# A four-layer graph-attention kernel: two ties at a layer border, row stores on another queue, a last half by position, a root on GpSimd

## The chip, the cores and the metric

The kernel runs on one core of one Trainium2 chip. The metric is the device time of one execution in microseconds, the median of several. The times here are 2258.48, 2259.3 and 2261.46 us.

## The reference

A graph of N = 4096 nodes with F = 256 features passes four attention layers. Each layer is followed by a residual sum and a layer norm: `x = layernorm(x + layer(x))`. The adjacency matrix is random with density 1/256 and a full diagonal, so that a node has some 17 neighbours. Layers 0 and 1 have four heads, layer 2 has two. The last layer, which the change touches most, is

```python
h = x @ W
e = leaky_relu(h @ a[:F] + (h @ a[F:]).T, 0.2)
attention = softmax(where(adj > 0, e, -1e12), axis=1)
negative = -softmax(where(adj > 0, -e, -1e12), axis=1)
out = elu(concatenate([attention @ x, negative @ x], axis=1) @ fc_W)
x = layernorm(x + out)        # (x - mean) / sqrt(var + 1e-5)
```

## The kernel before

**Tiling.** The nodes form 32 row tiles of 128. For each row tile, a first stage packs the neighbours of its 128 rows into 13 tiles of gathered nodes; with the tile's own rows this makes NP = 14 positions, two halves of HALF = 7. For a layer, every node has a row in DRAM (`vals`), made by the `Projection` (L529) of the layer before: the transposed row block times the weights, with the steps transpose, copy, multiply, row (which stores `vals` at L583), edge (a transpose on PE, L587) and store (L595).

**A row tile** (`RowTile`, L604). `load` (L630) fetches in half 0 the attention terms S (L635) and the mask mk (L637), in half 1 the residual rows y (L1012), all on SP's queue. Of the 14 positions it gathers 13 by GpSimd's indirect DMA (L645); position FRONT = 6 is the tile's own rows and comes by a plain load on SP (L642). `place` (L613) gives each position a slot of a pool that other tiles use again. `half` (L649) computes, in layer 3, seven Relus of 128x128 on ScalarE (L686), an Exp of 128x896 (L687), a multiplication by the mask on VectorE (L688), a second Exp (L689), a second multiplication (L690), and 14 matmuls on TensorE (L723) into two banks. `finish` (L741, L1060) scales the two sums (L1054, L1057, L1074 to L1076), applies the ELU (L1079 to L1082, with an Exp on ScalarE at L1080) and calls `norm` (L1015): statistics (L1022, L1023), variance plus epsilon (L1031), the inverse root by a bit trick (L1033, L1034) and three Newton steps of four instructions each (L1038 to L1041), the scaling of the row (L1043), and its store on SP's queue (L1045). In layer 3 the store goes to the output.

**Whole rows.** In layers 2 and 3 some blocks of four row tiles are not gathered: they are computed against all 32 node tiles. In layer 3 these are rows 28 to 31, in 64 units of four matmuls (L993), each with a Relu (L985), an Exp (L987 or L989), a mask (L990) and a load of node rows (vw, L970). The other 28 row tiles (0 to 27) go by gather. The units are spread over the steps (`whole`), with AHEAD = 10 of them before the first half.

**Order.** A scheduler orders the instructions of each engine by priority within the program's data dependences, and each engine executes its own list in order; that holds of SP's queue, too, whose list is loads and stores. `tc.issue_after(ins)` pins the instructions of a block behind `ins` on the engine of `ins`. `half_with_whole` (L839) is one step of layers 2 and 3: the half of a tile, projections, the finish of the tile before, units.

**The border.** `close` (L889) ends a layer. Between layers 2 and 3 it loads the first four tiles of layer 3, runs five of its units, finishes the last row tile of layer 2, projects it, pins tile 0's first half and five more units behind the scaling of that row (on VectorE) and the last transpose of its projection (on TensorE), and calls tile 1's first half without a pin. At the end of layer 3 it runs the units that are left and finishes tile 27.

Of the kernel before, what the change touches and what calls it, by code (L numbers as in the profile page):

```python
# [37 lines left out]
F32 = mybir.dt.float32  # L38
# [6 lines left out]
AF = mybir.ActivationFunctionType  # L45
ALU = mybir.AluOpType
# [4 lines left out]
P = 128  # L51
# [4 lines left out]
BT = 4  # L56
# [17 lines left out]
HALF = NP // 2  # L74
# [10 lines left out]
WIDTH = (65, 65, 129, 257)  # L85
VALS = tuple(h * w for h, w in zip(HEADS, WIDTH))
# [4 lines left out]
TERMS = tuple(a + b for a, b in zip(LOGS, EXPS))  # L91
# [8 lines left out]
AHEAD = 10  # L100
# [38 lines left out]
@with_exitstack  # L139
def kernel(ctx: ExitStack, tc: tile.TileContext, ins: dict, out: bass.AP):  # L140
    nc = tc.nc
    const = ctx.enter_context(tc.tile_pool(name="const", bufs=1))
    dram = ctx.enter_context(tc.tile_pool(name="xs", bufs=1, space=DRAM))
    ident = const.tile([P, P], F32, name="ident")
    make_identity(nc, ident)
    shared = {
        "ident": ident,
        "idx": const.tile([P, NT, NP], I32, name="idx"),
        "flag": const.tile([1, 1], I32, name="flag"),
        "shift1": const.tile([P, 1], F32, name="shift1"),  # L150
        "shift2": const.tile([P, 1], F32, name="shift2"),
        "shift3": const.tile([4, 4], F32, name="shift3"),
        "zero": const.tile([4, 4], F32, name="zero"),
        "maskC": dram.tile([NT, P, NP, MC], U8, name="maskC"),
        "maskW": dram.tile([NB, P, NT, BT, MC], U8, name="maskW"),
        "d": [const.tile([P, NT, TERMS[n]], F32, name=f"d{n}") if WHOLE[n] else None for n in range(4)],
        "v": [dram.tile([N, ROW[n]], F32, name=f"vals{n}") for n in range(4)],
        "e": [dram.tile([NT, TERMS[n], P], F32, name=f"edge{n}") for n in range(4)],
        "x": [None] + [dram.tile([N, F], F32, name=f"xp{n}") for n in (1, 2, 3)],
    }  # L160
    nc.vector.memset(shared["shift1"], -KEXP)
    nc.vector.memset(shared["shift2"], -2.0 * KEXP)

    nc.vector.memset(shared["zero"], 0.0)
    nc.vector.memset(shared["shift3"], -2.0 * KEXP)
    nc.gpsimd.affine_select(out=shared["shift3"], in_=shared["shift3"], pattern=[[1, 4]], compare_op=ALU.is_gt,
                            fill=0.0, base=0, channel_multiplier=-1)
    with ExitStack() as packed:
        Program(tc, packed, ins, out, shared).run()
    general = nc.values_load(shared["flag"][0:1, 0:1], min_val=0, max_val=1,  # L170
                             skip_runtime_bounds_check_because="it is the result of a comparison")
    with tc.If(general > 0):
        dense_layers(tc, ins, out, ident)
# [430 lines left out]
class RowTile:  # L604
# [44 lines left out]
    def half(self, half):  # L649
# [32 lines left out]
            return G[k][:, V + T + h:V + T + h + 1]  # L682

        if n == 3:
            for k in range(HALF):
                nc.scalar.activation(w[0][:, k, :], S[:, 0, :], AF.Relu, bias=d(k, 0))  # L686
            nc.scalar.activation(w[1], w[0], AF.Exp, scale=-1.0)  # L687
            nc.vector.tensor_tensor(w[1], w[1], mh, op=ALU.mult)  # L688
            nc.scalar.activation(w[0], w[0], AF.Exp, bias=sh["shift2"])  # L689
            nc.vector.tensor_tensor(w[0], w[0], mh, op=ALU.mult)  # L690
            heads = (1, 0)
        else:
            for h in range(A, T):
                k = 0
                while k < HALF:
                    pos = half * HALF + k
                    e = 2 if pos % 2 == 0 and k + 1 < HALF else 1
                    if e == 2:
                        dd = self.slots[pos // 2][:, :2 * ROW[n]].rearrange("p (t c) -> p t c", t=2)
                        nc.vector.tensor_tensor(  # L700
                            w[h][:, k:k + 2, :], S[:, h:h + 1, :].to_broadcast([P, 2, P]),
                            dd[:, :, V + T + h:V + T + h + 1].to_broadcast([P, 2, P]), op=ALU.mult)
                    else:
                        nc.vector.tensor_scalar(w[h][:, k, :], S[:, h, :], d(k, h), None, op0=ALU.mult)
                    k += e
            for h in range(A):
                for k in range(HALF):
                    nc.scalar.activation(w[h][:, k, :], S[:, h, :], AF.Exp, bias=d(k, h))  # L708
                if n == 2:
                    nc.vector.scalar_tensor_tensor(w[h], w[h], LEAST, mh, op0=ALU.max, op1=ALU.mult)  # L710
                elif h % 2 == 0:
                    masked(pairs[h // 2])
            heads = list(range(A, H)) + list(range(A))
        for h in heads:
            for k in range(HALF):
                pos = half * HALF + k
                how = dict(start=pos == 0 and (n == 3 or h == heads[0]), stop=pos == NP - 1, skip_group_check=True)
                v = G[k][:, h * Wd:(h + 1) * Wd]
                if n < 2:
                    nc.tensor.matmul(accs[0][:Wd, h * P:(h + 1) * P], v, w[h][:, k, :], **how)  # L720
                else:
                    a = accs[h][:, :Wd] if n == 3 else accs[0][:, h * Wd:(h + 1) * Wd]
                    nc.tensor.matmul(a, w[h][:, k, :], v, **how)  # L723

    def copy(self):

# [19 lines left out]
class Layer:  # L746
# [3 lines left out]
    def __init__(self, prog, n):  # L750
        self.prog, self.n, self.nc, self.shared = prog, n, prog.nc, prog.shared
        self.order = ORDER[n]
        self.count = len(self.order)
        self.tiles = {}
        self.loaded = set()
        self.units = self.whole_rows()
        self.total = len(WHOLE[n]) * NT * (1 if n < 3 else 2)
        self.used = self.ahead = 0
        self.nxt = self.middle = self.between = None
        self.stored = []  # L760
        self.group = []
        self.ready = []
        self.step = 0
        self.last = ()
# [74 lines left out]
    def half_with_whole(self, m, part):  # L839
# [12 lines left out]
        with ExitStack() as order:  # L852
            for ins in self.last:
                order.enter_context(self.prog.tc.issue_after(ins))
            self.last = ()
            if part == 1 or self.tile(m).accs is None:
                self.tile(m).half(part)
        if self.between is not None:

            self.last = self.between()  # L860
            self.between = None
# [8 lines left out]
        for proj in projs:  # L870
            proj.row()
            proj.edge()
        self.stored = projs

    def steps(self):
        for m in range(self.count):
# [12 lines left out]
    def close(self, following):  # L889
# [16 lines left out]
        if WHOLE[self.n]:  # L906
            for _ in self.units:
                pass
            if following is None:
                self.tile(last).finish()  # L910
                return


            following.ahead = AHEAD
            self.project_ready()
            for _ in range(AHEAD // 2):
                following.unit()
            self.tile(last).finish()
            scaled = self.scaled
# [1 line left out]
            with ExitStack() as order:  # L921
                for ins in (scaled, proj.last):
                    order.enter_context(self.prog.tc.issue_after(ins.ins))
                following.tile(0).half(0)
                for _ in range(AHEAD - AHEAD // 2):
                    following.unit()
        else:
            self.set_banks()
            first = Projection(self.prog, self.n + 1, self.nxt, *self.ready.pop(0)[1:])
# [11 lines left out]
        if following is not None:  # L941
            for m in (1, 2):
                following.load(m, 0)
            following.tile(1).half(0)
            following.load(3, 0)


# [67 lines left out]
    def norm(self, y, m):  # L1015
# [13 lines left out]

        v = ep.tile([P, BT], F32, name="v")[:, :g]  # L1030
        nc.vector.tensor_scalar(v, mv[:, :, 1], EPS, None, op0=ALU.add)  # L1031
        b = ep.tile([P, BT], I32, name="b")[:, :g]
        nc.vector.tensor_scalar(b, v.bitcast(I32), 1, None, op0=ALU.logical_shift_right)  # L1033
        nc.vector.tensor_scalar(b, b, -1.0, float(0x5F3759DF), op0=ALU.mult, op1=ALU.add)  # L1034
# [2 lines left out]
        for _ in range(3):  # L1037
            nc.vector.tensor_tensor(u, r, r, op=ALU.mult)  # L1038
            nc.vector.tensor_tensor(u, u, v, op=ALU.mult)  # L1039
            nc.vector.tensor_scalar(u, u, -0.5, 1.5, op0=ALU.mult, op1=ALU.add)  # L1040
            nc.vector.tensor_tensor(r, r, u, op=ALU.mult)  # L1041
        for i, (y, m) in enumerate(self.group):
            self.scaled = nc.vector.tensor_scalar(y, y, mv[:, i, 0:1], r[:, i:i + 1], op0=ALU.subtract, op1=ALU.mult)  # L1043
            dst = self.prog.out if self.n == 3 else self.shared["x"][self.n + 1]
            nc.sync.dma_start(out=dst[m * P:(m + 1) * P, :], in_=y)  # L1045
            if self.n < 3:
                self.ready.append((self.step + 1, y, m))
        self.group = []

# [495 lines left out]
```

## Time and profile before

| what | value |
|---|---|
| median of three runs | 2259.3 us |
| profiled execution, own time | 2261.27 us |
| profiled execution, span | 2259.5 us |
| mean granted TensorE clock | 0.963 of full speed |
| busy: PE, PEld | 2020.2, 1842.9 us |
| busy: DVE, ACT, POOL | 1786.0, 1730.1, 1493.1 us |
| 1456 gathers (L645) on POOL | 1480.1 us busy, 1017 ns each |
| layer 3, first full gather to the end | 1767.8 to 2259.5 us |

The profile is one execution, and its times are microseconds from the start of the span. PE is TensorE's matmuls, PEld its weight loads, DVE VectorE, ACT ScalarE, POOL GpSimd, SP SyncE; SPq is SP's queue of DMAs. In a line of a group or timeline, `w<-S,G` says that a tile named w is written from S and G; L686 is line 686 of the kernel before. Idle time in brackets, as in `[8.56 <-DMA G<-vals]`, is the time that the engine stood ahead of the instruction, and what released it. The ends of matmuls are modelled, and POOL's spans are rough. All four layers use every engine, so a share of the whole span says little on the last layer.

### The profile page before, as it was taken

How to read it: one execution, taken by the hardware profiler on the slowest of the kernel's cores; microseconds unless marked ns; L12 is line 12 of the kernel's file. 1: busy time of each engine (PE TensorE's matmuls, PEld its weight loads, DVE VectorE, ACT ScalarE, POOL GpSimd, SP SyncE). 2: the span in 40 equal slices, each digit the busy share in tenths (PEclk: the TensorE clock that was granted, in tenths of full speed). 3: DMA queues.
4: the chain of work that ended last, by engine and by line, in shares of the span. 5: the costliest groups of instructions: out<-in, count | busy, mean ns of one | idle time of the engine just before them, and what ended most of it. 6: DMA issues, size and time to landing. Idle time of an engine off the chain costs nothing. (4 is left out here: it accounts for less than half of the span.)

```text
span 2259.5 us, 49108 instructions
## 1 busy us (share of the span) xinstructions
PE 2020.2 (89%) x15689; PEld 1842.9 (82%) x15689; DVE 1786.0 (79%) x5061; ACT 1730.1 (77%) x4977; POOL 1493.1 (66%) x1596
## 2 busy tenths in 40 slices
PE   4878888989999969989889898999998999899995
PEld 2658878878899859988889798999997888788784
DVE  2888999999999859888889786887976466655566
ACT  4777988988789859978889767987875666666653
POOL 2107656656667777777777777777773477777773
PEclk7898999999999979999999999999999999999998
DMA  8779868776567666666666666778777688898874
GB/s 283 250 242 357 281 214 255 251 245 225 147 169 193 178 197 171 180 179 168 175 182 168 171 166 182 211 216 235 227 220 212 197 281 273 261 284 261 260 239 122
DMA packets 250319, 492.99 MB, mean 218 GB/s; under 512 B 44385, under 2 KB 156610, under 8 KB 249666
## 3 DMA queue, kind: packets, MB, share of 16 engines
q0 software_dynamic: 81536, 245.30, 38.4%
q1 hardware_dynamic: 168514, 244.46, 33.7%
q8 instruction: 126, 2.06, 0.4%
q14 instruction: 143, 1.17, 0.2%
HBM read 437.05 MB, written 52.54 MB: 217 GB/s over the span
## 5 line engine op out<-in xcount | busy, mean ns | idle before, releaser
L645 POOL DMA_INDIRECT G<-vals,idx x1456 | 1480.1, 1017 | 723.2 <-issue 225.1
L708 ACT ACTIVATE w<-S,G 128x128 f32<-128x128 f32 x3248 | 1000.1, 390 | 137.9 <-DMA G<-vals,idx 99.6
L720 PE MATMUL bank<-w,G 128*65 128x128 f32 x7168 | 840.7, 277 | 61.0 <-DVE w L679 61.0
L720 PEld LDWEIGHTS bank<-w,G 128*65 128x65 f32 x7168 | 801.9, 141 | 70.8 <-DVE w L679 69.5
L679 DVE SCALAR_TENSOR_TENSOR w<-w,bank 128x1792 f32<-128x1792 f32 x256 | 514.7, 2014 | 16.6 <-ACT w L708 14.2
L723 PE MATMUL bank<-G,w 128*128 128x257 f32 (+1 forms) x2688 | 495.7, 342 | 33.7 <-ACT z L1057 21.6
L723 PEld LDWEIGHTS bank<-G,w 128*128 128x128 f32 x2688 | 436.0, 195 | 82.7 <-ACT z L1057 26.1
L993 PE MATMUL bank<-vw,pw 128*128 128x129 f32 (+1 forms) x2048 | 301.2, 304 | 1.8 <-issue 1.8
L993 PEld LDWEIGHTS bank<-vw,pw 128*128 128x128 f32 x2048 | 276.4, 193 | 17.8 <-issue 2.3
L686 ACT ACTIVATE w<-S,G 128x128 f32<-128x128 f32 x392 | 137.2, 391 | 148.6 <-DMA G<-vals 94.6
L438 DVE TENSOR_SCALAR oh<-iota,place 128x256 bf16<-128x256 f16 (+2 forms) x992 | 222.6, 300 | 9.7 <-PE bank L444 9.7
L700 DVE TENSOR_TENSOR w<-S,G 128x256 f32<-128x256 f32 x384 | 152.4, 417 | 69.9 <-DMA G<-vals,idx 66.8
L444 PE MATMUL bank<-mk,oh 128*128 128x132 fp8e4 x2336 | 191.3, 227 | 15.6 <-DVE oh L438 9.3
L555 PE MATMUL bank<-wext,xT 128*128 128x268 f32 (+3 forms) x640 | 180.8, 416 | 15.6 <-ACT xT L546 12.8
L444 PEld LDWEIGHTS <-oh 128*128 128x128 bf16 x2336 | 147.6, 99 | 51.0 <-DVE oh L438 16.2
L383 ACT ACTIVATE mk<-raw 128x1024 uint8<-128x1024 int32 x128 | 130.5, 1051 | 29.6 <-DMA raw<-in_adjB_dram 29.6
L555 PEld LDWEIGHTS bank<-wext,xT 128*128 128x128 f32 x640 | 119.6, 204 | 35.4 <-ACT xT L546 15.6
L983 DVE SCALAR_TENSOR_TENSOR pw<-pw,mw 128x512 f32<-128x512 f32 x192 | 127.4, 689 | 18.0 <-ACT pw L982 17.7
L982 ACT ACTIVATE pw<-Sw,d 128x512 f32<-128x512 f32 x192 | 133.0, 709 | 8.6 <-PE bank L993 5.5
L688 DVE TENSOR_TENSOR w<-w,mk 128x896 f32<-128x896 f32 x56 | 61.0, 1090 | 96.3 <-ACT w L687 87.6
L710 DVE SCALAR_TENSOR_TENSOR w<-w,mk 128x896 f32<-128x896 f32 x80 | 86.7, 1087 | 39.8 <-ACT w L708 39.6
L451 ACT ACTIVATE cm<-bank 128x396 uint8<-128x396 f32 (+1 forms) x160 | 69.0, 452 | 47.4 <-PE bank L444 46.3
(130 smaller groups left out, 1519.3 us busy)
## 6 DMA issues: line engine op xcount, KB each, us to landing
raw<-in_adjB_dram SPq DMA_DIRECT2D x128, 512.0 KB
mk<-maskC SPq DMA_DIRECT2D x112, 231.0 KB
G<-vals,idx POOLq DMA_INDIRECT x1456
S<-edge SPq DMA_DIRECT2D x64, 256.0 KB
vw<-vals SPq DMA_DIRECT2D x96, 129.0 KB
xp<-y SPq DMA_DIRECT2D x96, 128.0 KB
y<-xp SPq DMA_DIRECT2D x96, 128.0 KB
mw<-maskW SPq DMA_DIRECT2D x20, 528.0 KB
```

The lines of the kernel that those rows point to most:

```text
L438: nc.vector.tensor_scalar(oh[:, :n * P], iota[:, :n * P], self.place[:, it, j:j + 1], None, op0=ALU.is_equal)
L444: nc.tensor.matmul(accs[b][:, s * MC:(s + 1) * MC], oh[:, (k - a) * P:(k - a + 1) * P], mk[:, j, it, :].bitcast(FP8), start=touches[b][0] ...
L555: nc.tensor.matmul(pp[:, :c1 - c0], self.xT[:, k, :], wext[:, k, c0:c1], start=(k == 0), stop=(k == KT - 1 and brow is None))
L645: nc.gpsimd.indirect_dma_start(out=self.place(pos), out_offset=None, in_=sh["v"][n][:NODES[t], :], in_offset=bass.IndirectOffsetOnAxis(ap= ...
L679: nc.vector.scalar_tensor_tensor(pair, pair, LEAST, mh2, op0=ALU.max, op1=ALU.mult)
L686: nc.scalar.activation(w[0][:, k, :], S[:, 0, :], AF.Relu, bias=d(k, 0))
L700: nc.vector.tensor_tensor(w[h][:, k:k + 2, :], S[:, h:h + 1, :].to_broadcast([P, 2, P]), dd[:, :, V + T + h:V + T + h + 1].to_broadcast([P ...
L708: nc.scalar.activation(w[h][:, k, :], S[:, h, :], AF.Exp, bias=d(k, h))
L720: nc.tensor.matmul(accs[0][:Wd, h * P:(h + 1) * P], v, w[h][:, k, :], **how)
L723: nc.tensor.matmul(a, w[h][:, k, :], v, **how)
L982: nc.scalar.activation(p, S[:, h], AF.Exp, bias=d)
L993: nc.tensor.matmul(accs[it][:, c:c + Wd], p[:, it, :], v[:, c:c + Wd], start=(j == 0 and h == heads[0]), stop=(j == NT - 1), skip_group_ch ...
```

## The change

1. A constant tile `mhalf` of -0.5 is added, with one memset.
2. At the border of layers 2 and 3, three units instead of five run ahead of the last row's finish, seven instead of five behind it, and tile 1's first half is pinned behind the same two instructions as tile 0's.
3. The 32 output rows of layer 3 are stored by ScalarE's queue instead of SP's. They are issued behind the second Exp of a following half; those that are left at the end are issued before and after the finish of the last tile.
4. The second half of tile 27, the very last half, goes position by position: Relu, two Exps and two multiplications on 128x128 and two matmuls for each of the seven positions.
5. The inverse root of row tile 27 is one GpSimd instruction, `pow` of 128x1 by -0.5, instead of the bit trick and the Newton steps on VectorE.

```diff
@@ half
         if n == 3:
+            if half == 1 and self.step == L.count - 1:
+                return self.last_half(accs, G, w, mh)
...
-            nc.scalar.activation(w[0], w[0], AF.Exp, bias=sh["shift2"])
+            self.exps = nc.scalar.activation(w[0], w[0], AF.Exp, bias=sh["shift2"])
...
+    def last_half(self, accs, G, w, mh):
+        nc, sh, Wd = self.layer.nc, self.layer.shared, WIDTH[3]
+        V, T = VALS[3], TERMS[3]
+        for k in range(HALF):
+            d = G[k][:, V + T:V + T + 1]
+            nc.scalar.activation(w[0][:, k, :], self.S[:, 0, :], AF.Relu, bias=d)
+            nc.scalar.activation(w[1][:, k, :], w[0][:, k, :], AF.Exp, scale=-1.0)
+            nc.vector.tensor_tensor(w[1][:, k, :], w[1][:, k, :], mh[:, k, :], op=ALU.mult)
+            nc.scalar.activation(w[0][:, k, :], w[0][:, k, :], AF.Exp, bias=sh["shift2"])
+            nc.vector.tensor_tensor(w[0][:, k, :], w[0][:, k, :], mh[:, k, :], op=ALU.mult)
+            for h in (1, 0):
+                nc.tensor.matmul(accs[h][:, :Wd], w[h][:, k, :], G[k][:, h * Wd:(h + 1) * Wd],
+                                 start=False, stop=k == HALF - 1, skip_group_check=True)
@@ half_with_whole
             if part == 1 or self.tile(m).accs is None:
                 self.tile(m).half(part)
+                if self.outs:
+                    order.enter_context(self.prog.tc.issue_after(self.tile(m).exps.ins))
+                    self.store_rows()
...
+    def store_rows(self):
+        for y, m in self.outs:
+            self.nc.scalar.dma_start(out=self.prog.out[m * P:(m + 1) * P, :], in_=y)
+        self.outs = []
@@ close
             if following is None:
+                self.store_rows()
                 self.tile(last).finish()
+                self.store_rows()
                 return
...
-            for _ in range(AHEAD // 2):
+            for _ in range(3):
                 following.unit()
             self.tile(last).finish()
...
                 following.tile(0).half(0)
-                for _ in range(AHEAD - AHEAD // 2):
+                for _ in range(AHEAD - 3):
                     following.unit()
+                following.tile(1).half(0)
...
-            following.tile(1).half(0)
+            if not WHOLE[self.n]:
+                following.tile(1).half(0)
@@ norm
         nc.vector.tensor_scalar(v, mv[:, :, 1], EPS, None, op0=ALU.add)
+        if self.n == 3 and m == self.order[-1]:
+            r = ep.tile([P, BT], F32, name="r")[:, :g]
+            nc.gpsimd.tensor_tensor(r, v, self.shared["mhalf"][:, :g], op=ALU.pow)
+            self.scale(mv, r)
+            return
...
+    def scale(self, mv, r):
...
-            dst = self.prog.out if self.n == 3 else self.shared["x"][self.n + 1]
-            nc.sync.dma_start(out=dst[m * P:(m + 1) * P, :], in_=y)
-            if self.n < 3:
+            if self.n == 3:
+                self.outs.append((y, m))
+            else:
+                nc.sync.dma_start(out=self.shared["x"][self.n + 1][m * P:(m + 1) * P, :], in_=y)
                 self.ready.append((self.step + 1, y, m))
```

More of the change, by code (lines that the diff above doesn't have):

```diff
@@ L148 @@
         "idx": const.tile([P, NT, NP], I32, name="idx"),
+        "mhalf": const.tile([P, BT], F32, name="mhalf"),
         "flag": const.tile([1, 1], I32, name="flag"),
@@ L160 @@
     }
+    nc.vector.memset(shared["mhalf"], -0.5)
     nc.vector.memset(shared["shift1"], -KEXP)
@@ L873, in half_with_whole @@
         self.stored = projs
+    def store_rows(self):
+        for y, m in self.outs:
+            self.nc.scalar.dma_start(out=self.prog.out[m * P:(m + 1) * P, :], in_=y)
+        self.outs = []
     def steps(self):
@@ L1041, in norm @@
             nc.vector.tensor_tensor(r, r, u, op=ALU.mult)
+        self.scale(mv, r)
+    def scale(self, mv, r):
+        nc = self.nc
         for i, (y, m) in enumerate(self.group):
             self.scaled = nc.vector.tensor_scalar(y, y, mv[:, i, 0:1], r[:, i:i + 1], op0=ALU.subtract, op1=ALU.mult)
-            dst = self.prog.out if self.n == 3 else self.shared["x"][self.n + 1]
-            nc.sync.dma_start(out=dst[m * P:(m + 1) * P, :], in_=y)
-            if self.n < 3:
+            if self.n == 3:
+                self.outs.append((y, m))
+            else:
+                nc.sync.dma_start(out=self.shared["x"][self.n + 1][m * P:(m + 1) * P, :], in_=y)
                 self.ready.append((self.step + 1, y, m))
```

## The prediction

> **What bounds the kernel now.** The change touches only layer 3, its border with layer 2, and the end, so whole-span shares decide nothing. I first read the waits of all engines from 1800 us on, then busy time by stretch, then SP's queue, and last the timelines of the border and of the end. Columns of a wait line: engine, what waited, what it waited for, us in total, times, longest.
>
> ```profile
> ACT w L686 <- DMA G<-vals: 94.6, 17, 8.6
> DVE w L688 <- ACT w L687: 75.8, 16, 9.9
> POOL G L645 <- PE bank L723: 36.2, 115, 1.1
> PE bank L723 <- ACT z L1057: 21.6, 10, 7.8
> ```
>
> ScalarE loses most, 94.6 us, waiting for the plain load of a tile's own rows (FRONT, L642). GpSimd's 115 waits are almost all the 0.30 us that separates any two gathers. Only two exceed 0.35 us in layer 3 after 1783: 0.73 at 1802.5 and 1.05 at 1956.8.
>
> ```profile
> 1860.00:1880.00 20.00, 20.00 (x94) 17.57 (x93) 11.14 (x30) 12.51 (x27) 15.29 (x16) 1.00 0.88 276
> 2000.00:2020.00 20.00, 20.00 (x94) 17.57 (x93) 12.14 (x34) 12.86 (x30) 15.43 (x16) 1.00 0.87 259
> ```
>
> The columns after the length are PE, PEld, DVE, ACT, POOL, PE clock, DMA share, GB/s. POOL's 15.3 of 20 us look idle but are full: 16 gathers at 0.95 + 0.30 = 1.25 us. A tile needs 13, so 16.25 us. PE needs 56 L723 and 16 L993 per tile at 0.222 us, 16.0 us. Both limits lie together, but only POOL never pauses: **the gather stream paces layer 3**, and ScalarE's 94.6 us are mostly paid in slack.
>
> SP's queue shows where FRONT is held:
>
> ```profile
> SPq L635 <- ACT w L686: 145.1, 23, 10.5
> SPq L1045 <- DVE y L1043: 122.4, 26, 22.5
> ```
>
> The store L1045 stands 122.4 us for the row norm, and FRONT is issued right behind it. At the end this costs time:
>
> ```profile
> 2204.14 0.34 SPq L1045 DMA_DIRECT2D out_dram<-y  x1
> 2204.65 0.90 SPq L642 DMA_DIRECT2D G<-vals  x2
> ```
> ```profile
> 2212.31 0.69 ACT L686 ACTIVATE w<-S,G 128x128 f32<-128x128 f32 x2 [8.56 <-DMA G<-vals]
> ```
> ```profile
> 2216.82 26.77 PE L723 MATMUL bank<-G,w 128*128 128x257 f32 x112 [7.80 <-ACT z L1057]
> ```
> ```profile
> 2225.38 0.95 POOL L645 DMA_INDIRECT G<-vals,idx  x1 [0.30 <-PE bank L723]
> ```
> ```profile
> 2253.26 0.41 DVE L1043 TENSOR_SCALAR y<-y,mv,b 128x256 f32<-128x256 f32 x1
> ```
>
> Store at 2204.14, FRONT issued 2204.65 and landed about 7 us later; ScalarE stands 8.56 us, and z of tile 24, queued behind on ScalarE, is late; PE, whose bank z must free, stands 7.8 us and resumes at half clock. PE then runs 112 matmuls (tiles 26 and 27) to 2243.6, 17 us after the last gather. DVE's chain of rows 26 and 27 ends 2253.67, and store and finish take 5.8 us to 2259.5.
>
> The border:
>
> ```profile
> 1745.55 1.09 DVE L688 TENSOR_TENSOR w<-w,mk 128x896 f32<-128x896 f32 x1 [6.50 <-ACT w L687]
> 1746.56 0.16 DVE L1069 RECIPROCAL rec<-bank 128x2 f32<-128x2 f32 x1
> ```
> ```profile
> 1764.33 0.32 SPq L583 DMA_DIRECT2D vals<-row  x1
> ```
> ```profile
> 1767.78 0.94 POOL L645 DMA_INDIRECT G<-vals,idx  x1 [22.93 <-DMA vals<-row]
> 1782.83 1.41 POOL L645 DMA_INDIRECT G<-vals,idx  x1 [3.77 <-PE bank L723]
> ```
> ```profile
> 1770.26 8.83 PE L993 MATMUL bank<-vw,pw 128*128 128x257 f32 x40
> 1778.93 6.23 PE L723 MATMUL bank<-G,w 128*128 128x257 f32 x28
> ```
>
> Layer 2's last row waits on DVE behind layer 3's masking (L688, tile 1 half 0), so projection, its store (1764.33) and the first full gather (1767.78) are late. Nine gathers on, POOL waits 3.77 us for slots that tile 1's half 0 frees.
>
> [...] SP's L1045 stood 122.4 us, FRONT behind it. The same will now hold of ScalarE. [...] seven L686 of 128x128 take 2.3 us where an Exp of seven times the width takes 0.95. [...]
>
> **The change part by part.**
> *Border.* Nothing is removed: two of ten units move behind the projection, and tile 1's half 0 behind that. The instruction lists show 12 L993 instead of 20 ahead of the last projection's transpose, and 28 instead of 20 between tile 0's half and tile 1's. The pin takes DVE's wait away: L1069 comes once its sums stand, about 2.7 us earlier by its PE matmuls. The other 2.6 us are PE's eight matmuls less, 8 x 0.222 = 1.8 us, and their masks. So the last row's store moves from 1764.33 to about 1759.0, 5.3 us. But tile 1's half 0 now comes behind 28 L993 after tile 0's half, not 20: what PE saves ahead of the projection (1.8 us) it pays here, and the two units' Relus, Exps and masks with it (2.2 us). Of the 5.3 us it keeps 1.3: its start moves from 1778.93 to 1777.6, and the tenth gather, bound to it, gains that only. The later waits of 0.73 and 1.05 us lose 0.43 + 0.75 beyond the usual 0.30. Sum **2.5 us** on the gather stream; ends 0 (slots still bind) and 5.3 (all of it).
>
> *Stores.* 32 stores leave SP; ScalarE issues them behind the second Exp of a later half. SP's stores cost 0.34 us each, so 28 in the loop take 9.5 us of ScalarE over 480, beside its 94.6 us of waits: nothing on the path; without that cover, 0.34 us per tile. Added is the wait for L1043 on ScalarE. Queued behind it are the next half's L686, and for those wait DVE, PE and the gathers' slots. From 1862.58 (z, L1057) to the norm's end 1870.38 are 7.8 us; the ScalarE work between them in the new order (seven L686, two Exps, two L1080) takes about 6.3 us, so the stand is **1.5 us a tile**, against 4.7 to 8.6 for FRONT now. Loop: 7.8 for z to norm, 0.4 issue, 6.2 for 28 matmuls and 0.3 for L1054 make 14.7 us, under POOL's 16.25. FRONT stays behind S and mask loads (L635, L637) on SP; these wait for the tile before, which is early enough. The y load (L1012) waits for a store's landing (63.9 us in 23 waits on SP) as now. Through mid-layer this gains nothing, POOL paces. At the end it counts: ScalarE's 8.56 us stand goes, PE goes on at 2209. What is late next is z of tile 25, queued on ScalarE after two positions of the last half, about 2223.4 (2.5 us gather shift included); PE then starts tile 27 at 2223.4 instead of 2231.2 and ends 2235.9 instead of 2243.6.
>
> *Last half by position.* 2 Exps and 2 mults of 128x896 become 14 and 14 of 128x128. ScalarE: 21 x 0.3 = 6.3 us instead of 2.3 + 1.9 = 4.2, but spread under the gathers' arrival and tile 27's half 0 on PE. The last mult comes at about 2230.5 (before: 2237.4), 6.9 us earlier, the FRONT stall included. The small mults push into DVE some of the norms of rows 28 to 31; behind the last mult about 3.9 us of that remain, instead of 3.1: **-0.8**.
>
> *The root.* L1033 to L1041 of row 27, 14 instructions, run 2250.57 to 2253.26, 2.7 us; a GpSimd pow replaces them. No row shows it. [...] I take 1.1, with the hand-over both ways: the nearest POOL row, a gather, is 0.95. Gain **+1.6** [...].
>
> *Waits added at the end.* Four stores of rows 28 to 31 stand ahead of z of tile 26 on ScalarE, one ahead of z of tile 27: only the last of each is exposed, about 0.25 each: **-0.5**.
>
> Sum on DVE's final chain: 6.9 - 0.8 + 1.6 - 0.5 = **7.2 us**; L1043 ends 2246.5 instead of 2253.67, PE's end 2235.9 is no limit. The profiled execution (span 2259.5, its own time 2261.27) becomes 2254.1; it lay 2.0 us above the median of 2259.3, so the median becomes **2252.1**.
>
> **The rivals.** I take 0.2% (4.5 us) as what a measurement can tell from no change; faster is below 2254.8, slower above 2263.8.
> 1. *One stall for another.* ScalarE's stand for the store or z of tile 25 takes the place of FRONT's at the end; only the root's 1.6 us and some border stay: about 2257. For it: the same in-order engine carries both. Against: 1.5 us is less than 4.7 to 8.6. The instruction lists show the edits do reach the engines, so a change without effect would be this one too.
> 2. *Slower: ScalarE's store stand bounds PE.* PE needs 16.0 of each 16.25 us. Now it loses some 33 us in layer 3 (26 us of waits for z and half-clock time), 1.2 us a tile over 27 tiles. If the stands at the stores delay the Relus so that PE loses more than that, the end comes later; at 1.5 us, all of the stand, it is 0.3 x 27 = 8 us later, less the root's 1.6: 2265.7. It decides from 1.2 us a tile.
> 3. *More:* the gather stream keeps the border's whole 5.3 us (+2.8) and the root costs next to nothing (+1): with 2 to 3 us more from a PE that keeps its clock, about 2246.
>
> **How the numbers follow.** Forecast 0.58, rival 1 0.16, rival 2 0.12, rival 3 0.14. The forecast's own range: the gather shift of 0 to 5.3 moves it by +2.5 and -2.8, [...]: 2248 to 2256. A tenth of it lies above 2254.8. Faster: 0.52 + 0.14 + a fifth of rival 1 = 0.69; same 0.19; slower 0.12. Range 2244.5 to 2260: it leaves out rival 2 and the far end of rival 3.
>
> **What would show it.** Right: ScalarE's wait for FRONT in layer 3 falls from 94.6 to under 30 us; PE's 7.8 us gap at 2209 goes; the last gather starts at about 2222.9; last row's store at the border about 1759; the pow near 1 us; final L1043 ends near 2246.5. Wrong: gathers in layer 3 with waits over 1 us again and again, ScalarE's stores standing over 3 us a tile, or a pow of several us.

## The result, and the profile after

The changed kernel takes 2254.28 us (median of 7 runs) against 2260.61 us for the kernel before in the same runs: 6.3 us less, ratio 0.9964, 95% interval 0.9952 to 0.9976. Single runs of a kernel scatter by 2 to 5 us (standard deviation), on the slower chip of the last four experiments by 6 to 12. The profiled execution of the changed kernel, with its span of 2249.3 us and own time of 2251.02, is the fastest of its seven; its 10.2 us against the span of before overstate the gain, so the trace is used for where the time went and the medians for how much.

The lines of the changed kernel have moved: FRONT's load is L644, gathers L647, Relu and Exps L690, L691, L693, masks L692, L694, matmuls of a half L727 (of the very last half L741), units L1027, z L1102, scaling L1087, the store on ScalarE L902, the pow L1069, the `vals` store L585.

First the waits of all engines from 1800 us on (engine, what waited, for what, us in total, times, longest):

```profile
ACT w L690 <- DMA G<-vals,idx: 62.8, 72, 2.8
...
POOL G L647 <- PE bank L727: 31.4, 103, 0.3
...
ACT w L690 <- DVE y L1087: 30.2, 14, 4.0
...
PE bank L727 <- ACT z L1102: 13.6, 6, 5.6
...
ACT w L690 <- DMA G<-vals: 13.0, 6, 3.6
```

ScalarE's wait for FRONT is 13.0 us, was 94.6. In its place stand two: 30.2 us behind the stores, which wait for the scaling of a row (2.2 us each in 14 waits), and 62.8 us for the gathers. From 1800 us on no gather waits over 0.31 us: GpSimd's stream paces ScalarE.

The border, in the timelines of SP, GpSimd and TensorE:

```profile
1756.72 0.32 SPq L585 DMA_DIRECT2D vals<-row  x1
```
```profile
1760.48 0.95 POOL L647 DMA_INDIRECT G<-vals,idx  x1 [16.88 <-DMA edge<-erow]
...
1778.68 0.95 POOL L647 DMA_INDIRECT G<-vals,idx  x1 [7.24 <-PE bank L727]
```
```profile
1762.65 12.30 PE L1027 MATMUL bank<-vw,pw 128*128 128x257 f32 x56
1774.78 6.23 PE L727 MATMUL bank<-G,w 128*128 128x257 f32 x28
```

This profile was 1.25 us ahead of before already at layer 2's last gather (1742.66, was 1743.91). Counted from there, the row's store came 6.4 us earlier and the first full gather 6.0, but the wait of the tenth gather grew from 3.77 to 7.24 us, so that it came only 2.9 us earlier. The PE lines show why: ahead of tile 1's first half 56 records of units stand in one row, against 40.

The end, in the timelines of TensorE, GpSimd, VectorE and ScalarE's queue:

```profile
2203.21 14.51 PE L727 MATMUL bank<-G,w 128*128 128x257 f32 x56 [5.63 <-ACT z L1102]
2219.61 6.33 PE L727 MATMUL bank<-G,w 128*128 128x257 f32 x28 [1.89 <-ACT z L1102]
2225.78 6.23 PE L741 MATMUL bank<-G,w 128*128 128x257 f32 x28
```
```profile
2218.53 1.04 POOL L647 DMA_INDIRECT G<-vals,idx  x1 [0.30 <-issue]
2238.81 0.58 POOL L1069 TENSOR_TENSOR r<-v,mhalf 128x1 f32<-128x1 f32 x1 [19.23 <-DVE v L1065]
```
```profile
2239.42 0.41 DVE L1087 TENSOR_SCALAR y<-y,mv,r 128x256 f32<-128x256 f32 x1 [0.70 <-POOL r L1069]
```
```profile
2239.87 0.34 ACTq L902 DMA_DIRECT2D out_dram<-y  x1
```

TensorE takes up tile 26 at 2203.2, 15.3 us ahead of the last gather (before 8.6), and its last matmul ends at 2232.0, 13.5 us behind it (before 18.2). The last row doesn't wait for that: its z starts on ScalarE at 2235.62, when VectorE is through with row 26. The last scaling ends at 2239.83, 21.3 us behind the last gather (before 28.3). But from there to the span's end pass 9.5 us, where before it was 5.8. The 10.2 us of this profile are 1.25 ahead of the border, 5.6 in the gather stream, 7.0 between last gather and last scaling, less 3.6 given back at the very end.

### The profile page after: what moved, and what is told of

Read it like the earlier page. It is cut to its first block, busy times and chain, and to the rows that moved or that the text cites. A ratio compares the mean times of both kernels' runs of the same rounds, so it can differ in the third digit from the quotient of the medians.

```text
span 2249.3 us, 49137 instructions
## 1 busy us (share of the span) xinstructions
PE 2014.0 (90%) x15689; PEld 1834.3 (82%) x15689; DVE 1786.6 (79%) x5060; ACT 1737.9 (77%) x4989; POOL 1494.4 (66%) x1597
## 5 line engine op out<-in xcount | busy, mean ns | idle before, releaser
L647 POOL DMA_INDIRECT G<-vals,idx x1456 | 1480.7, 1017 | 715.7 <-issue 221.1
L727 PE MATMUL bank<-G,w 128*128 128x257 f32 (+1 forms) x2660 | 490.8, 342 | 25.7 <-ACT z L1102 13.6
L727 PEld LDWEIGHTS bank<-G,w 128*128 128x128 f32 x2660 | 431.9, 195 | 73.2 <-ACT z L1102 16.4
L1027 PE MATMUL bank<-vw,pw 128*128 128x129 f32 (+1 forms) x2048 | 298.5, 301 | 3.7 <-issue 2.3
L1027 PEld LDWEIGHTS bank<-vw,pw 128*128 128x128 f32 x2048 | 273.6, 191 | 20.1 <-issue 2.8
L690 ACT ACTIVATE w<-S,G 128x128 f32<-128x128 f32 x385 | 137.8, 393 | 136.8 <-DMA G<-vals,idx 90.0
L1017 DVE SCALAR_TENSOR_TENSOR pw<-pw,mw 128x512 f32<-128x512 f32 x192 | 127.6, 689 | 18.2 <-ACT pw L1016 17.5
L1024 DVE TENSOR_TENSOR pw<-pw,mw 128x512 f32<-128x512 f32 x64 | 43.6, 691 | 85.4 <-ACT pw L1023 48.0
L692 DVE TENSOR_TENSOR w<-w,mk 128x896 f32<-128x896 f32 x55 | 60.0, 1091 | 59.5 <-ACT w L691 58.2
```

Of the source, the lines that this page charges most:

```text
L647: nc.gpsimd.indirect_dma_start(out=self.place(pos), out_offset=None, in_=sh["v"][n][:NODES[t], :], in_offset=bass.IndirectOffsetOnAxis(ap= ...
L1027: nc.tensor.matmul(accs[it][:, c:c + Wd], p[:, it, :], v[:, c:c + Wd], start=(j == 0 and h == heads[0]), stop=(j == NT - 1), skip_group_ch ...
```

## The experiments

The theory: the gather stream paces layer 3; the stores took FRONT, and with it the end, off that pace; the border moves the stream, the pow gives back what it saves (A). Rivals stand with each run. Runs e1 to e4 share one chip, e5 to e8 another, e9 to e12 a third. This table reads every profile by the same four marks, in us: layer 2's last gather to the tenth gather of layer 3, to the last gather, last gather to the end of the last scaling, last scaling to the end of the span.

| run | parts of the change | to tenth gather | to last gather | to last scaling | to the end | ratio to before, 95% |
|---|---|---|---|---|---|---|
| before | none | 38.9 | 481.5 | 28.3 | 5.8 | |
| after | all | 36.0 | 475.9 | 21.3 | 9.5 | 0.9964 (0.9952 to 0.9976) |
| e5 | all, again | 36.2 | 476.9 | 20.5 | 9.5 | 0.9970 (0.9958 to 0.9983) |
| e1 | no pow | 36.2 | 479.9 | 22.8 | 4.5 | 0.9970 (0.9957 to 0.9982) |
| e6 | no pow, again | 36.4 | 475.5 | 24.4 | 4.7 | 0.9960 (0.9949 to 0.9972) |
| e2 | idle pow | 36.5 | 479.7 | 22.0 | 7.4 | 0.9978 (0.9968 to 0.9988) |
| e3 | stores on SP | 36.5 | 480.4 | 27.5 | 9.4 | 1.0006 (0.9993 to 1.0019) |
| e4 | old border | 39.0 | 481.2 | 21.9 | 9.6 | 0.9978 (0.9968 to 0.9987) |
| e7 | old last half | 36.2 | 478.4 | 24.5 | 9.8 | 0.9983 (0.9972 to 0.9995) |
| e8 | stores alone | 37.7 | 481.2 | 26.4 | 4.5 | 0.9990 (0.9974 to 1.0005) |
| e9 | all, pow on row 26 | 36.3 | 528.1 | 22.9 | 4.7 | 0.9973 (0.9949 to 0.9997) |
| e10 | all, pow on 25, 31, 26 | 36.2 | 533.9 | 23.6 | 4.8 | 0.9982 (0.9957 to 1.0006) |
| e11 | stores and last half | 38.7 | 533.4 | 22.0 | 4.6 | 0.9994 (0.9980 to 1.0009) |
| e12 | last half alone | 38.8 | 528.4 | 25.8 | 5.9 | 0.9993 (0.9975 to 1.0010) |

The last four ran on a chip on which the kernel before took 2760.1 us (median of 59 runs), so their gather stream and their ratios don't compare with the rest; only their end is read. The premise of theory A fails there: the mean granted clock in their profiles was 0.89 to 0.90 (0.96 to 0.97 in the others), and 25 to 32 gathers after the tenth waited over 0.35 us, up to 5.8, where the other profiles have none to two. So the gathers don't keep their own pace; what sets it isn't shown.

**e1 and e6, without the pow; e2, an idle pow.**

```diff
-        if self.n == 3 and m == self.order[-1]:
-            r = ep.tile([P, BT], F32, name="r")[:, :g]
-            nc.gpsimd.tensor_tensor(r, v, self.shared["mhalf"][:, :g], op=ALU.pow)
-            self.scale(mv, r)
-            return
```

In e2 the pow stays, into a tile that nothing reads, and the row takes Newton's steps.

> The changed kernel with row 27's root back on VectorE (two bit-trick instructions and three Newton steps); all else kept. In the changed kernel the span ends 9.1 us after the last scaling, before the change 5.8 us. Theory A (GpSimd's own end does it: its pow makes it the last engine to reach the closing drain, which takes 6.4 us): the last scaling ends 2.0 us later, but the time from there to the end falls from 9.1 to about 5 us; the span is 2 to 3 us shorter than the changed kernel's, and the median some 2.5 us below it. Theory B (the last store on ScalarE's queue, with its branch behind it, makes the end longer): 9.1 us stay, and the kernel is 2.0 us slower than the changed one.

> As the kernel without the pow, but a GpSimd pow on row 27's variance is still issued, and its result is used by nobody. Theory A (GpSimd's end): the pow alone brings back a late end; the last scaling ends with the kernel without pow, but the span ends 9 to 10 us after the pow, about where the changed kernel ends and 2 to 3 us after the kernel without pow. Theory B (ScalarE's last store): the same time as the kernel without pow, within 0.5 us.

> The kernel without the pow once more, on the same chip as the changed kernel. Its first run showed 4.5 us from the last scaling to the end against 9.5, and a last scaling 1.5 us later against the last gather, so theory A expects 2 to 3.5 us less than the changed kernel; the rival that the pow costs nothing in the whole (some other end, such as the program's start or close outside the span, takes up what it frees) expects the same time within 1 us.

The end behind the last scaling falls from 9.5 to 4.5 and 4.7 us, though the last store is still on ScalarE: theory B falls. It is even shorter than before. With the stores on SP and no late pow it takes 5.8 and 5.9 us (before, e12), with the stores on ScalarE 4.5 to 4.8 (e1, e6, e8 to e11): moving them also brings some 1.2 us at the very end. Why isn't shown. The DRAIN records, the last of which start on each engine 0.2 to 0.6 us ahead of the span's end (2249.3 and 2252.3), say who is last. Of the changed kernel (engine, count, min/median/max ns, first and last start):

```profile
L1586 POOLq DRAIN  x3: 44/107/6443, 2242.0 to 2249.0; - x3
...
L1586 ACTq DRAIN  x2: 8/8/8, 2243.6 to 2248.7; - x2
```

and of e1:

```profile
L1580 POOLq DRAIN  x3: 44/113/10295, 2222.2 to 2252.1; - x3
...
L1580 DVEq DRAIN  x2: 10/14/17, 2251.2 to 2251.8; - x2
L1580 ACTq DRAIN  x2: 8/8/8, 2251.4 to 2251.8; - x2
```

With the pow, GpSimd reaches its drain at 2242.0 and needs 6.44 us, to 2248.5; ScalarE had come to its first at 2243.6, and its second starts at 2248.7, behind GpSimd's long one. Without, GpSimd's drain runs from 2222.2 to 2232.5 under the other work, and ends 6.4 us behind the end of the last gather (2226.0). In all six runs with a pow on row 27 the span ended 10.4 to 10.8 us after the pow's start, e2 included, where nobody reads it. So the late end is shown to be the pow's. In the profiles it costs 4.9 us at the end and saves 1.5 to 3.8 on the chain from last gather to last scaling, of which 2.0 by its own lines; in e6 1.6 of the rest is one store that took long (see e7). The times don't settle the net: on one chip e6 is 2.3 us below e5 (mean of 22 runs each; 95% by resampling 4.8 less to 0.4 more), while e1's ratio is that of e5. The idle pow cost 1.2 us over e1, within its scatter (1.2 less to 3.4 more).

**e3, stores back on SP.**

```diff
-                self.outs.append((y, m))
+                self.nc.sync.dma_start(out=self.prog.out[m * P:(m + 1) * P, :], in_=y)
```

> The changed kernel with layer 3's row stores back on SP's queue, issued where the row is scaled; border, last half and pow as in the changed kernel. Theory A (the stores held FRONT, and FRONT held the end): ScalarE's wait for FRONT is back at over 70 us in layer 3, the last scaling comes about 25 us after the last gather instead of 20.9, and the median is 4 to 5 us above the changed kernel's. Theory C (the border's earlier gather stream gave most, and the last half by position shortens the end): within 1.5 us of the changed kernel.

Its waits, from 1780 us on:

```profile
ACT w L690 <- DMA G<-vals: 89.0, 17, 8.9
ACT w L690 <- DMA G<-vals,idx: 32.8, 48, 2.4
PE bank L727 <- ACT z L1102: 20.8, 10, 6.9
```

The wait for FRONT is back at 89.0 us, with the 8.9 us stand, and the last scaling moves from 21 to 27.5 us behind the last gather. The ratio is 1.0006: with border, last half and pow, but without the stores, nothing is left of the gain. Theory A holds, and the cost (7.6 us by the medians, 8 to 9.5 by the ratios) is above the 4 to 5 expected. Two limits: the pow's late end (9.4 us) is in this run as well, and border and last half without stores and without pow weren't run; and FRONT isn't the only load behind the stores on SP. A run with FRONT alone moved off that queue would settle the second.

**e4, the border of before.**

```diff
-            for _ in range(3):
+            for _ in range(AHEAD // 2):
...
-                for _ in range(AHEAD - 3):
+                for _ in range(AHEAD - AHEAD // 2):
                     following.unit()
-                following.tile(1).half(0)
...
-            if not WHOLE[self.n]:
-                following.tile(1).half(0)
+            following.tile(1).half(0)
```

> The changed kernel with the border of before (five units, five units, tile 1's first half not pinned); the rest as changed. Theory A (the gather stream paces layer 3 and the tail follows it): the tenth gather comes about 2.9 us later against the last gather of layer 2, the last gather 3 to 5.6 us later, and the median is 3 to 5 us above the changed kernel's. Theory D (the border's gain is eaten by the slots of tile 1, or the tail is bound by VectorE's chain): 0 to 1 us.

The tenth gather is back at 39.0 and the last at 481.2 us. Over the seven profiles with the new border on chips of the usual speed the last gather lies at 475.5 to 480.4, mean 478.1; over the three with the old one at 481.2 to 481.5. So the border moves the stream by about 3.2 us, with more scatter than the old one has. The ratios put e4 1.8 to 3.2 us above the changed kernel, which didn't run on e4's chip, and their intervals overlap. The shift of the stream is shown; in the time it is of the expected sign, at or below the low end of the expected 3 to 5 us, and hardly clear of noise.

**e5, the changed kernel again.**

> The changed kernel once more, beside the variants, since single runs scatter by several us. Theory A: from the last scaling to the end again 9 us or more; ratio to before about 0.9964; the last gather between 476 and 481 us after the last gather of layer 2.

It repeats: 9.5 us at the end, 476.9, ratio 0.9970.

**e7, the last half in one piece; e8, the stores alone.** e7:

```diff
-            if half == 1 and self.step == L.count - 1:
-                return self.last_half(accs, G, w, mh)
```

e8 takes e7 and puts border and root back as well.

> The changed kernel with the very last half as two Exps and two multiplications of 128x896, as before; stores, border and pow as changed. The prediction has the small instructions hidden beside tile 27's first half on TensorE, at some 0.8 us of added work on VectorE: so within 1.5 us of the changed kernel either way, the last scaling 20 to 23 us after the last gather. Rival: the position-wise half is what brings TensorE's end forward, then the last scaling comes 3 us or more later.

> The kernel before with the row stores on ScalarE's queue alone: border, last half and root of before. Theory A: the stores carry most of the gain: the last scaling 22 to 24 us after the last gather instead of 28.3, the end 4.5 to 5.8 us behind it, a median 5 to 6.5 us below before (ratio 0.9971 to 0.9978). Rival: the stores need the position-wise half to pay, then under 3 us.

Both miss. e7 is 2.7 us slower than e5 on the same chip (0.2 to 5.3), the last scaling 3.2 to 4 us later behind the last gather. Its rival has the size, but not the reason: TensorE ends 13.7 us behind the last gather, against 13.5 in the changed kernel's first profile. e8 keeps 4.2 us of the 6.3 by the medians, but 2.3 by its ratio, whose interval doesn't exclude that nothing is gained; and it has 26.4 us to the last scaling, not 22 to 24. The timelines of e7 show the place, on VectorE and ScalarE:

```profile
2227.98 1.08 DVE L692 TENSOR_TENSOR w<-w,mk 128x896 f32<-128x896 f32 x1
2232.71 0.41 DVE L1085 TENSOR_SCALAR y<-y,mv,b 128x256 f32<-128x256 f32 x1
```
```profile
2226.84 1.04 ACT L691 ACTIVATE w<-w,shift 128x896 f32<-128x896 f32 x1
2231.99 2.83 ACTq L900 DMA_DIRECT2D out_dram<-y  x4
2234.87 0.47 ACT L1100 ACTIVATE z<-bank,recp 128x256 f32<-128x256 f32 x1 [6.99 <-DMA out_dram<-y]
```

(Lines of e7 are two less than the changed kernel's.) The same place in the changed kernel:

```profile
2225.01 0.28 DVE L739 TENSOR_TENSOR w<-w,mk 128x128 f32<-128x128 f32 x1
2228.14 0.41 DVE L1087 TENSOR_SCALAR y<-y,mv,b 128x256 f32<-128x256 f32 x1
```
```profile
2223.98 0.40 ACT L738 ACTIVATE w<-w,shift 128x128 f32<-128x128 f32 x1
2227.04 1.88 ACTq L902 DMA_DIRECT2D out_dram<-y  x4
2228.97 0.47 ACT L1102 ACTIVATE z<-bank,recp 128x256 f32<-128x256 f32 x1 [4.59 <-DMA out_dram<-y]
```

And on VectorE in the kernel before (L690 is its last mask, L1043 the scaling):

```profile
2236.31 1.08 DVE L690 TENSOR_TENSOR w<-w,mk 128x896 f32<-128x896 f32 x1
2239.08 1.39 DVE L1043 TENSOR_SCALAR y<-y,mv,b 128x256 f32<-128x256 f32 x4
```

The way from last gather to last scaling falls into four pieces, in us: to the end of the last mask; from there to the last scaling of rows 25 and 29 to 31, whose norms lie together (row 28 is normed with row 24, earlier); to the start of z of tile 26, which stands on ScalarE behind the stores of these four rows; and through rows 26 and 27 to the last scaling.

| run | last mask | four rows scaled | z of tile 26 | rows 26 and 27 |
|---|---|---|---|---|
| before | 12.0 | 3.1 | 0.4 | 12.8 |
| e3, stores on SP | 13.5 | 3.1 | 0.2 | 10.8 |
| e8, stores alone | 7.2 | 4.1 | 2.2 | 12.9 |
| e7, old last half | 7.8 | 4.1 | 1.7 | 10.9 |
| after | 6.8 | 3.3 | 0.4 | 10.9 |
| e6, no pow | 6.2 | 3.3 | 2.0 | 12.9 |

The first piece is the stores' gain: on the chips of the usual speed it is 12 us and more with them on SP, 5 to 8 with them on ScalarE. The second is the last half's: the Newton chains of the four rows lie behind the two large masks in e7 and e8, and between small masks they go ahead, which brings 0.8 us; and the last mask itself comes 1.0 us later in e7 than in the changed kernel's first profile. The third is something else. A store's issue takes 0.34 to 0.45 us on ScalarE, but one of the four ahead of z of tile 26 took 1.3 to 2.0 us in e4, e6, e7 and e8, with small masks and with large. The issues of all 32 stores, in e7 and then e1 (min/median/max ns):

```profile
L900 ACTq DMA_DIRECT2D out_dram<-y x32: 338/338/1469, 1807.1 to 2245.8; - x32
```
```profile
L902 ACTq DMA_DIRECT2D out_dram<-y x32: 338/338/444, 1809.6 to 2247.9; - x32
```

So 1.3 us of e7's lag and some 1.8 of e8's 26.4 us aren't shown to come from the last half, and that the stores need it to pay is only in part borne out.

**e9 and e10, the pow elsewhere.** e9 and then e10:

```diff
-        if self.n == 3 and m == self.order[-1]:
+        if self.n == 3 and m == self.order[-2]:
```
```diff
-        if self.n == 3 and m == self.order[-1]:
+        if self.n == 3 and m in (self.order[-3], self.order[-2], NT - 1):
```

> The changed kernel with the GpSimd pow moved one row on: the root of row tile 26 by pow, the very last row 27 by Newton's steps on VectorE. In six runs with a pow on row 27 the span ended 10.4 to 10.8 us after the pow's start, whatever else was changed. Row 26's pow starts some 7.7 us before the last scaling, so its end falls before that of the other engines. Theory A expects the 2.0 us saved on VectorE without the late end: the last scaling 21 to 22.5 us after the last gather, the span's end 4.5 to 4.8 us behind it, and a median 3 to 5 us under the changed kernel's and some 2 us under the one without pow (ratio to before about 0.995). Rival: the end after the last scaling stays over 7 us, then the late end is not the pow's place.

> As the run before, with pow also for the two groups of rows normed just ahead (those that end with rows 25 and 31), so that VectorE loses three Newton chains in the tail, and only row 27 keeps its own. Theory A: VectorE's in-order chain is what sets the last scaling, so it comes another 1 to 3 us earlier (18.5 to 21 us after the last gather), the end again 4.5 to 4.8 us behind it. Rival: in this version the four stores of rows 28 to 31 stand on ScalarE ahead of the last position's Exps, and hold TensorE's end by as much as the chains save: no gain over the run before, or a loss of 1 to 2 us.

e9's pow, one row ahead, leaves the end at 4.7 us:

```profile
2729.65 0.58 POOL L1069 TENSOR_TENSOR r<-v,mhalf 128x1 f32<-128x1 f32 x1 [11.42 <-DVE v L1065]
```
```profile
L1586 POOLq DRAIN  x3: 44/107/6443, 2733.1 to 2744.7; - x3
...
L1586 ACTq DRAIN  x2: 8/8/8, 2744.1 to 2744.4; - x2
```

GpSimd's drain is over at 2739.5, ScalarE's comes at 2744.1: the rival falls. The saving on the chain doesn't show, since TensorE ended only at 2733.7 on this chip and row 27 waited for it. e10's rival holds in the trace, as ScalarE's timeline shows (the medians, 2754.2 us against e9's 2752.0, don't separate the two):

```profile
2728.73 2.41 ACTq L902 DMA_DIRECT2D out_dram<-y  x4
2731.19 0.31 ACT L736 ACTIVATE w<-w 128x128 f32<-128x128 f32 x1 [2.12 <-DVE w L739]
```

Four stores stand ahead of the last position's Exp and hold it by 2.1 us; TensorE ends 17.1 us after the last gather, e9 16.5.

**e11, stores and last half; e12, the last half alone.** e11 is e1 with the border of before, e12 is e11 with the stores on SP, by the diffs above.

> Before with two parts of the change: row stores on ScalarE's queue and the last half by position; border and root of before. With the stores alone the last scaling came 26.4 us after the last gather; with stores, border and last half it came 22.8 and 24.4. If the two parts need each other, this run shows 22 to 24.5 us, the end 4.5 to 4.8 us behind, and a median 4 to 6 us under before; if the border is the third party, 26 us and 2 to 3 us under before.

> Before with the last half by position alone: stores on SP, border and root of before. If it pays only once the stores are off SP's queue, the last scaling comes 27 to 29.5 us after the last gather (before 28.3) and the median is within 1.5 us of before. Rival: it pays by itself, 3 us or more.

e11 has 22.0 us from last gather to last scaling, without the border and the pow, much like e1 and e6. e12 has 25.8, below its expected range. The kernel before left no profile on this chip, so its 28.3 us don't compare; against each other the two runs give the stores 3.8 us here: TensorE ends 11.9 us behind the last gather in e11, 19.3 in e12, where row 27 waits for it. The ratios, 0.9994 and 0.9993, separate neither from before on that chip, where the stream from tenth to last gather takes 490 us and more instead of 440; the expected 4 to 6 us of e11 are missed. How much the two bring there, and whether e9 beats the kernel without the pow on a chip of the usual speed, stays open.

## Why the prediction was right, and where not

The forecast was 2252.1 us for 2259.3, 7.2 us less; measured were 6.3 us less by the medians. Direction and size hold, the size in part by luck. Against the sum, the gather stream gave 3.2 us for 2.5 and the way from last gather to last scaling 7.0 and 7.8 (after, e5) for 4.7, while the end took 3.7 that the sum doesn't have. By its steps:

- **The border.** Forecast: row's store 5.3 us earlier, tenth gather 1.3, stream 2.5. The profile: 6.4, 2.9, and 3.2 on average over the profiles. The slots of tile 1 bind as said (3.77 grew to 7.24 us). Right, somewhat small.
- **The stores.** FRONT's wait under 30 us: 13.0. ScalarE's stand 1.5 us a tile: 2.2 in 14 waits. The sum behind the 1.5 is off: the work that it lists takes 5.1 us in the trace of before (seven Relus 2.3, two Exps 2.0, two Exps of the ELU 0.8), not 6.3, and with z's own 0.5 that leaves 2.2 of the 7.8. Nothing gained in mid-layer: GpSimd paces before and after. e3 shows that beside the pow nothing is gained without this part. The 7.8 us gap of PE was to go; 5.6 us of it remain, at z of the tile two before, which now stands on ScalarE behind a half that waits for its gathers and not for FRONT. Against the last gather TensorE is still 6.8 us ahead of where it was. The half clock behind the gap stays as well: 0.50 from 2216.8 to 2220.0 before, 0.50 from 2203.2 to 2206.4 after.
- **The last half by position.** The last mask was to come 4.4 us earlier against the last gather (6.9 less the border's 2.5); it came 5.2 earlier. The step that failed: "the small mults push into DVE some of the norms", 3.9 us behind the last mult instead of 3.1, -0.8. Measured are 3.3 us, so the term is -0.2 (the four rows are 25 and 29 to 31, not 28 to 31). It is the large masks that push the norms back once the stall is gone: 4.1 us in e7 and e8. What was taken for a cost of 0.8 us is a gain, which e7 prices at 2.7 us (0.2 to 5.3), the long store of e7's trace aside.
- **The root.** The trace of before has no pow: the 1.1 us with the hand-over, and what the forecast's range allows for the root, were the author's estimate. The pow took 0.58 us; from variance to scaling 0.85 us, so 2.0 us were saved, forecast 1.6.
- **The waits added at the end.** Forecast -0.5, the author's estimate. In the changed kernel's profile nothing is lost there (0.4 us to z of tile 26, as before); in e4 and e6, with one long store, 1.0 and 1.7 us.
- **The end.** The step that failed: "store and finish take 5.8 us" was carried over to the changed kernel unexamined. There GpSimd had been done long before, its drain over at 2232.7 of 2259.5 us; the pow makes it last, and its drain of 6.44 us is on the path. 9.5 us pass instead of 5.8, and 4.5 to 4.7 without the pow, where the stores on ScalarE have brought 1.2 that the sum doesn't have either. The whole forecast holds since the late end nearly cancels what the stretch ahead of it gained beyond the sum.

Rival 1 (the stall only changes its name) holds in part: the store's stand and the gathers took FRONT's place, but at the gathers' pace. Rival 2 (ScalarE's stand bounds PE) doesn't: PE's waits for z from 1800 us on fell from 21.6 to 13.6 us. For the slower chip of e9 to e12 that isn't shown.

## What to carry to other kernels

Ask of every in-order queue what stands behind a store that waits for a slow chain; a load that others need shouldn't stand there, even where its wait is covered in mid-layer: here it cost its time at the end, where the cover was gone (ScalarE stood 8.56 us for FRONT at 2212.31 before, and the stores back on SP cost 7.6 us by the medians in e3). When an instruction is moved to an idle engine near the end, count that engine's own way to the end of its closing drain, not only the instruction: saved on the chain is not saved in the span (here 2.0 us by the pow's own lines, against 4.9 us at the end). Parts of a change should be priced together where one sets the order in which another's work falls (here, with nothing but the stores moved, the way from the last large mask to the four rows' scaling grew from 3.1 us in before to 4.1 in e8).

## What the hardware showed unexpectedly

- GpSimd's closing drain took 6.44 us with a pow in the tail (the changed kernel's profile and e9's), and started 2.6 and 2.9 us after the pow's end. Without a pow, too, it ended 6.4 us after the end of the last gather (e1: 2226.0 and 2232.5). The other engines' drains took 7 to 17 ns. In the six runs with a pow of 128x1 in the last row the span's end came 10.4 to 10.8 us after the pow's start, though the pow itself takes 0.54 to 0.72 us, and 0.89 on 128x3.
- The issue of a store took 0.34 to 0.45 us on ScalarE in most cases. But in the tail one or two took 0.9 to 2.0 us in six of the eleven profiles with the stores on ScalarE (after, e4, e6, e7, e8, e10), and what is queued behind it came later by that: in e6 the last scaling is 1.6 us later behind the last gather than in e1. On SP the longest of the 32 took 0.42 us in before. What stretches an issue isn't shown.
